# A Fourier-operator kernel on one NeuronCore: the order of the interleaved fc1 and fc2 steps, and the place of one addition, in the spectral mixing of layers 1 to 3

## The chip, the cores and the metric

The kernel runs on one core of one Trainium2 chip. The metric is the device time of one execution in microseconds (us); lower is better. The engines are TensorE (PE in the profile; PEld is its weight load), VectorE (DVE), ScalarE (ACT), GpSimd (POOL) and SyncE (SP, which here only issues DMAs). PSUM is the memory that TensorE writes and that VectorE and ScalarE empty[...].

## The reference, cut to what matters

Eight images of 8 channels, 256 x 256, in fp32. Each is normalised in 4 groups, goes through a small Fourier neural operator (4 layers, 4 groups of width 10, 12 x 12 complex modes), and then through fc1 (10 to 128 per group), a swish and fc2 (128 to 2 per group). The result is added to the image; a second normalisation and a 3 x 3 maximum follow.

```python
h = _gconv1x1(h, fc0_w, fc0_b)
for i in range(4):
    h1 = _spectral_conv(h, sp_w1[i], sp_w2[i])   # FFT, mix 12x12 modes over channels, inverse FFT
    h2 = _gconv1x1(h, w_w[i], w_b[i])
    h = h1 + h2
    if i < 3:
        h = _gswish(h, betas[i])
h = _gswish(_gconv1x1(h, fc1_w, fc1_b), betas[3])
return _gconv1x1(h, fc2_w, fc2_b)
...
x = x + _L0_conv_ref(_gn(x), ...)
x = x + _L1_conv_ref(_gn(x))                      # 3x3 maximum
```

## The kernel before, in words

**Two images at once.** The layers of image b and the head (fc1, swish, fc2, addition to x) of image b-1 run interleaved. The layers are written as generators. Each `yield` hands out a short string, and the main loop turns every letter of it into one step of the head of the image before. While image 0 is in its layers there is no such head, and the letters do nothing. A head has 128 fc1 steps and 64 fc2 steps.

**The letters** (function `step`, L839). `f` first issues all additions that are due (`sum_up`, L712) and then one fc1 step. `F` is one fc1 step without that. `C` is one fc2 step, whose addition is only put on the list `sums_due`; `c` is the same, with the additions issued directly behind it. `t` is a step of the 3 x 3 maximum of an earlier image.

**One fc1 step** (`first`, L743): 4 matmuls of 32 x 128 weights with 512 columns (8 records in the profile, since fp32 shows as two each) into a small accumulator of one PSUM bank (tag "one") and a large one of three banks (tag "tri"), L753. ScalarE empties these with two Silu activations, L754 (the small one) and L755 (the large one), into an `act` tile, of which there are 4. Every third step also issues the load of a piece of the stored state on SP's queue (L729).

**One fc2 step** (`second`, L758): 8 matmuls (16 records, L770) over the `act` tiles of two fc1 steps, into one small accumulator. **The addition** (`add`, L774) reads this accumulator on VectorE and adds it to the image's rows: L779, or L777 for every eighth. Every eighth is followed by statistics (L785) and a store on GpSimd's queue.

**The accumulators.** There are two buffers with tag "one" and two with tag "tri", shared by fc1, fc2 and the layers' own stages. Which of the two a tile gets is settled when the program is built; a matmul that gets a buffer waits for the last reader of its former content.

**The order of work.** PE, DVE, ACT and SP run in the order in which the program issues (`manual_schedule`, L860). So a step's place among the yields is its place in these queues.

**The mixing** (`mix`, L390) multiplies the 12 x 12 modes with the layer's complex weights. It is VectorE work: 6 pairs of a multiplication (L398) and a reduction (L401), then six small sums and differences (L416, L417). The counter `n` runs over these 12 operations, and for layers 1 to 3 the string handed out behind operation n is:

```python
elif n not in (0, 2, 6, 10):
    yield "CF" if n in (1, 4, 7, 9) else "f"
```

Behind the small sums stands `yield "fc"` (L418), and then TensorE's fold of the modes (L429). Ahead of the mixing stands `spectrum_h` (L353), whose strings are "fc", "f", "fc", "f", "fc", "f"; its last TensorE work, L379, lies between that last "f" and the mixing. `sum_up` runs in an `f` ahead of its fc1 step, so an addition put on the list at n = 1 is issued at n = 3.

Of the kernel before, what the change touches and what calls it, by code (L numbers as in the profile page):

```python
# [40 lines left out]
STEPS = 128  # L41
# [4 lines left out]
def fno_dilate_kernel(ctx: ExitStack, tc: tile.TileContext, a: dict, out: bass.AP):  # L46
# [17 lines left out]
    def ps_four(name):  # L64
        one, tri = ps_a(f"{name}_0"), ps_tri(f"{name}_1")
        return one, tri, [one] + [tri[:, i, :] for i in range(3)]

    def part(i):
        return slice(32 * i, 32 * i + 32)
# [5 lines left out]
    def load_x(b):  # L75
        for i in range(2):
            nc.sync.dma_start(turned[:, i], a["xw"][b, :, i])
# [89 lines left out]
    for i in range(2):  # L167
        for r in range(4):
            mm(p[part(r), 1, NO * G * i : NO * G * (i + 1)], fc0c[:, i, :], wbd[:, NO * r : NO * (r + 1), :],
               start=True, stop=True)  # L170
# [214 lines left out]
    def load_sw(l, k):  # L385
        t = sb.tile([128, G, 2 * WID, WID], F32, tag="sw", bufs=3)
        nc.sync.dma_start(t.rearrange("p g m i -> p (g m i)"), a["spw"][l, k])
        return t

    def mix(b, l, out_):  # L390

        s = [sb.tile([128, 3, 2, WID, G], F32, tag=f"S{i}", bufs=1, name=f"S{i}_{b}_{l}") for i in range(2)]
        bt, sw = out_["bt"], out_["sw"]
        for n in range(12):
            k, k2 = n // 4, n // 2 % 2
            pr = turned[:, 2, 1024 * k2 : 1024 * k2 + 800].rearrange("p (g m i) -> p g m i", g=G, i=WID)
            if n % 2 == 0:
                nc.vector.tensor_tensor(  # L398
                    pr, sw[k], bt[:, k2, k].unsqueeze(2).to_broadcast([128, G, 2 * WID, WID]), ALU.mult)
            else:  # L400
                nc.vector.tensor_reduce(  # L401
                    s[k2][:, k].rearrange("p s o g -> p (s o) g"),
                    pr.rearrange("p g m i -> p m g i"), AX.X, ALU.add,
                )
            if l == 0:
                if n % 2 or n > 7:
                    yield
            elif n not in (0, 2, 6, 10):
                yield "CF" if n in (1, 4, 7, 9) else "f"
            if n == 2 and l == 3 and b + 1 < n_img:  # L410
                load_x(b + 1)
        for i, (x, y, op) in enumerate((
                (s[0][:, :, 0], s[1][:, :, 1], ALU.subtract), (s[0][:, :, 1], s[1][:, :, 0], ALU.add),
                (s[1][:, :, 1], s[0][:, :, 0], ALU.subtract))):
            three = [t[:, :, :9].rearrange("p k (r o) g -> p k r (o g)", r=3) for t in (x, y)]
            nc.vector.tensor_tensor(fs[:, 0:3, i].rearrange("p r k o g -> p k r (o g)"), *three, op)  # L416
            nc.vector.tensor_tensor(fs[:, 3, i, :, 0], x[:, :, 9], y[:, :, 9], op)  # L417
        yield "fc"  # L418

        n_f = 6 * NO * G  # L420
        if l > 0:
            nc.vector.tensor_copy(fz[:, :, :, 24], cz[:, l])
        if l < 2:
            nc.vector.tensor_copy(fz[:, :, :, 25], cz[:, 4 if l == 0 else 3])
        one, tri, banks = ps_four(f"p_f_{b}_{l}")
        for term in range(2):
            for r in range(4):
                for q in range(4):
                    mm(banks[q][part(r), :n_f], fold[part(q), term, :],  # L429
                       fs[part(q), r, term : term + 2].rearrange("p t k o g -> p (t k o g)"),  # L430
                       start=term == 0, stop=term == 1)
        if l == 0:
            mr = out_["mr"]
            nc.vector.tensor_tensor(dc[:, 0:1], mr[:, 0:1], mr[:, 1:2], ALU.mult)
            out_["wcn"] = sb.tile([128, 32], F32, tag="wcn", bufs=1, name=f"wcn_{b}")
            nc.vector.tensor_scalar(out_["wcn"], wc, mr[:, 1:2], None, ALU.mult)
            for r in range(4):
                mm(one[part(r), n_f : n_f + NO * G], dc, wm[:, NO * r : NO * (r + 1), :], start=True, stop=True)
        cols = fz.rearrange("p o g c -> p (o g) c")
        nc.vector.tensor_copy(  # L440
            cols[:, :, 6:24].rearrange("p x (q c) -> p q c x", q=3),
            tri[:, :, :n_f].rearrange("p q (c x) -> p q c x", c=6))
        nc.vector.tensor_copy(
            cols[:, :, 0:6].rearrange("p x c -> p c x"), one[:, :n_f].rearrange("p (c x) -> p c x", c=6))
        if l == 0:
            nc.vector.tensor_tensor(
                fz[:, :, :, 24], one[:, n_f : n_f + NO * G].rearrange("p (o g) -> p o g", o=NO), cz[:, 0], ALU.add)
# [181 lines left out]
    def start(b, out_):  # L629
        if b < n_img:  # L630
            out_["sw"] = [load_sw(0, k) for k in range(3)]
            yield from spectrum_x(b, out_)
            yield from mix(b, 0, out_)

    def rest(b, then):
        c = 0 if b == 0 else NCH - 4
        for n, _ in enumerate(then):
            yield REST[b > 0][n]
            for _ in range(2 if b == 0 else 1):
                if c < NCH:  # L640
                    read_x(b + 1, c)
                    c += 1
        for i in range(c, NCH):
            read_x(b + 1, i)

    def layers(b, stored, d, then):

        for l in range(4):
            if l > 0:
                yield from spectrum_h(b, l, d)
                yield from mix(b, l, d)
            yield from rows_of(b, l, then)
            yield from layer(b, l, d, stored, then)
        yield "stored"
        yield from rest(b, then)
# [53 lines left out]
    def sum_up():  # L712

        while sums_due:
            sums_due.pop(0)()
# [123 lines left out]
    def step(kind):  # L839

        for i, (b, (done, first, second, _)) in enumerate(heads):
            if kind in "fF" and done[0] < STEPS:
                if kind == "f":
                    sum_up()
                return first()
            if kind in "cC" and 2 * done[1] < STEPS:
                second()
                if kind == "c" or 2 * done[1] == STEPS:
                    sum_up()
                if 2 * done[1] == STEPS:  # L850
                    heads.pop(i)
                    tails.append((dilate if b + 1 < n_img else dilate_last)(b, stats_of.pop(b)))
                return

    def tail():
        if tails and next(tails[0], tails) is tails:
            tails.pop(0)

    stats_of = {}
    with tc.manual_schedule(engines={PE, DVE, ACT, SP}):  # L860
        d = {}
        for _ in start(0, d):
            pass
        for b in range(n_img):
            stored = [dram.tile([128, NQ * PIX], F32, tag=f"hs{c}", name=f"stored_{b}_{c}") for c in range(NCH)]
            ahead, new, n_ready = {}, None, 0
            for n in layers(b, stored, d, start(b + 1, ahead)):
                if n == "ready":
                    if new is None:
                        if b + 1 < n_img:  # L870
                            stats_of[b] = sb.tile([128, 8, 6], F32, tag="bn_y", name=f"bn_y{b}")
                        else:
                            stats_of[b] = spare[:, 16384:16480].rearrange("p (n s) -> p n s", s=6)
                        new = head(b, stored, stats_of[b])
                    new[3](n_ready)
                    n_ready += 1
                elif n == "stored":
                    heads.append((b, new))
                    alone[0] = False
                else:  # L880
                    for kind in n or "":
                        if kind == "t":
                            tail()
                        elif heads:
                            step(kind)
            d = ahead
        while heads:
            for kind in "ffc":
                if heads:
                    step(kind)  # L890
            tail()
        for t in tails:
            for _ in t:
                pass
# [163 lines left out]
```

## Time and profile before

| what | value |
|---|---|
| median of 3 runs | 3826.1 us (3812.43 to 3826.25) |
| the profiled execution | 3819.83 us, span 3818.0 us |
| TensorE, weight load | 3567.4 us busy, 1299.9 us |
| VectorE, ScalarE | 2422.9 us, 2821.9 us |
| fc1: matmuls L753 | 1150.2 us busy, 8192 records |
| fc2: matmuls L770 | 1024.3 us busy, 8192 records |
| activations L755, L754 | 1493.3 us, 616.3 us, 1024 each |
| additions L779 | 392 with mean 683 ns (and 56 more for the last image) |
| mixing: L398, L401 | 188.7 us, 188.9 us, 192 each |

The profile is of one execution. A row of the page gives line, engine, operation, tiles and shapes, then busy time and the mean of one, then the idle time of the engine just ahead of these instructions and what ended it. Busy times of TensorE are of overlapping matmuls whose ends are modelled, so the distance between starts says more than a length. A timeline puts neighbouring instructions of one kind into one row, and shows the idle time only ahead of the first.

### The profile page before, as it was taken

To read this page: it belongs to the slowest core of one execution; us is meant where nothing else is said; L and a number is where in the kernel's file an instruction comes from. 1 tells how busy PE (TensorE), PEld (TensorE's weight loads), DVE (VectorE), ACT (ScalarE), POOL (GpSimd) and SP (SyncE) were. 2 spreads that over 40 slices of the span, in tenths; PEclk is the share of its full clock that TensorE was granted. 3 is DMA by queue.
4 is the path that set the end of the run, shared out by engine and by line. 5 is a ranking of instruction groups with operands and counts; after the bars stand their busy time and mean duration, and the time that the engine had idled before them with its cause. 6 is when DMAs were issued, how large, how long until landed. Compare 5 with 4: busy or idle time off the path is not lost.

```text
span 3818.0 us, 117724 instructions
## 1 busy us (share of the span) xinstructions
PE 3567.4 (93%) x53432; PEld 1299.9 (34%) x53432; DVE 2422.9 (63%) x3781; ACT 2821.9 (74%) x2919; POOL 117.1 (3%) x202
## 2 busy tenths in 40 slices
PE   5768999999999999999999999999999999999997
PEld 2323333333333333333333333333333333333222
DVE  6776665557775667756776577765777566772443
ACT  2435777777777777787777877777777777778986
POOL 1000000000000000000000000000000000000000
PEclk7878999999999999999999999999999999999998
DMA  3005111432225212362123512144222532225221
GB/s 87 15 31 191 49 45 47 147 113 62 73 84 174 82 57 70 99 193 61 49 67 111 185 56 66 53 150 138 59 73 66 174 91 67 67 67 178 79 86 49
DMA packets 114067, 344.91 MB, mean 90 GB/s; under 512 B 15984, under 2 KB 18480, under 8 KB 98144
## 3 DMA queue, kind: packets, MB, share of 16 engines
q1 hardware_dynamic: 95392, 276.32, 24.0%
q0 software_dynamic: 18176, 61.07, 5.0%
q8 instruction: 420, 6.88, 0.8%
q14 instruction: 79, 0.65, 0.1%
HBM read 213.33 MB, written 123.74 MB: 88 GB/s over the span
## 4 chain that ended last, share of the span: by engine, by line
PE 74%; DVE 14%; ACT 5%; issue 4%; DMA 2%; POOL 0%; ACTq 0%; DVEq 0%; POOLq 0%
PE p_fc L770 21%; PE p_fc L753 20%; PE p_z L551 9%; PE p_z L548 7%; PE p_d L516 7%; PE p_z L545 3%; DVE turned L499 3%; PE p_u L530 3%; DVE S L401 2%; ACT act L755 2%; DVE turned L398 2%; DVE y L779 2%; PE p_g L468 2%; DMA yin<-y_rows 2%; ACT act L754 1%
## 5 line engine op out<-in xcount | busy, mean ns | idle before, releaser
L755 ACT ACTIVATE act<-p_fc 128x1536 f32<-128x1536 f32 x1024 | 1493.3, 1458 | 0.0
L753 PE MATMUL p_fc<-hs,c_w 32*128 32x512 f32 x8192 | 1150.2, 626 | 50.1 <-ACT act L754 19.1
L770 PE MATMUL p_fc<-act,c_w 128*32 128x512 f32 x8192 | 1024.3, 602 | 8.2 <-DVE y L779 6.3
L754 ACT ACTIVATE act<-p_fc 128x512 f32<-128x512 f32 x1024 | 616.3, 602 | 417.7 <-PE p_fc L753 408.4
L499 DVE STREAM_TRANSPOSE turned<-h 128x1024 f32<-128x1024 f32 x528 | 632.3, 1225 | 183.0 <-ACT h L556 182.4
L556 ACT ACTIVATE h<-p_z 128x512 f32<-128x512 f32 (+1 forms) x528 | 512.0, 1021 | 226.5 <-PE p_z L551 226.5
L779 DVE TENSOR_TENSOR y<-p_fc,y 128x512 f32<-128x512 f32 x392 | 267.6, 683 | 589.1 <-PE p_fc L770 586.4
L753 PEld LDWEIGHTS p_fc<-hs,c_w 32*128 32x128 f32 x8192 | 363.3, 184 | 638.9 <-ACT act L754 269.8
L770 PEld LDWEIGHTS p_fc<-act,c_w 128*32 128x32 f32 x8192 | 226.5, 109 | 709.8 <-issue 323.1
L551 PE MATMUL p_z<-c_binv,zt 32*128 32x256 f32 x5632 | 411.7, 406 | 0.0
L548 PE MATMUL p_z<-h,c_wt 32*32 32x512 f32 x8448 | 374.3, 607 | 8.4 <-ACT act L754 4.2
L551 PEld LDWEIGHTS p_z<-c_binv,zt 32*128 32x128 f32 x5632 | 259.6, 187 | 311.6 <-issue 298.4
L516 PE MATMUL p_d<-turned,c_fw 32*32 32x480 f32 (+1 forms) x9216 | 308.3, 540 | 0.7 <-DVE turned L499 0.4
L520 ACT ACTIVATE turned<-p_d 128x1440 f32<-128x1440 f32 x144 | 183.1, 1271 | 90.2 <-PE p_d L516 87.0
L558 ACT ACTIVATE h<-p_z,c_bias 128x512 f32<-128x512 f32 (+1 forms) x176 | 186.6, 1111 | 77.9 <-PE p_z L551 77.8
L208 DVE COPY zt<-p_g 128x264 f32<-128x264 f32 x304 | 155.4, 610 | 70.3 <-PE p_g L468 52.7
L401 DVE TENSOR_REDUCE S<-turned 128x80 f32<-128x800 f32 x192 | 188.9, 984 | 5.9
L398 DVE TENSOR_TENSOR turned<-t,B 128x800 f32<-128x800 f32 x192 | 188.7, 983 | 0.9
L516 PEld LDWEIGHTS p_d<-turned,c_fw 32*32 32x32 f32 x9216 | 127.2, 103 | 165.9 <-issue 65.0
L359 DVE STREAM_TRANSPOSE turned<-zt 128x960 f32<-128x960 f32 x96 | 176.7, 1865 | 2.5
L548 PEld LDWEIGHTS p_z<-h,c_wt 32*32 32x32 f32 x8448 | 94.3, 103 | 188.8 <-DVE y L779 54.1
L530 PE MATMUL p_u<-turned,c_stack 128*32 128x480 f32 (+1 forms) x1152 | 136.7, 543 | 11.5 <-DVE turned L519 6.2
(186 smaller groups left out, 1704.2 us busy)
## 6 DMA issues: line engine op xcount, KB each, us to landing
stored<-h SPq DMA_DIRECT2D x88, 1024.0 KB
hs<-stored SPq DMA_DIRECT2D x352, 256.0 KB
t<-in_spw SPq DMA_DIRECT2D x96, 400.0 KB
yin<-y_rows POOLq DMA_DIRECT2D x56, 512.0 KB, 5.3
h<-in_xp SPq DMA_DIRECT2D x352, 48.0 KB
turned<-in_xw SPq DMA_DIRECT2D x16, 1024.0 KB
y<-in_x SPq DMA_DIRECT2D x56, 256.0 KB
y_rows<-y POOLq DMA_DIRECT2D x56, 256.0 KB, 2.5
```

Of the source, the lines that this page charges most:

```text
L398: nc.vector.tensor_tensor(pr, sw[k], bt[:, k2, k].unsqueeze(2).to_broadcast([128, G, 2 * WID, WID]), ALU.mult)
L401: nc.vector.tensor_reduce(s[k2][:, k].rearrange("p s o g -> p (s o) g"), pr.rearrange("p g m i -> p m g i"), AX.X, ALU.add,)
L499: nc.vector.transpose(dst[:, 2 * i : 2 * i + 2], h[:, c, 2 * i : 2 * i + 2].rearrange("p f (s x) -> p f s x", s=2))
L516: mm(banks[q][part(v % 4), : 240 * n], fw8[part(q), v, :], t[part(q), :, :, v, : NBLK * WID], start=v < 4, stop=v >= 4)
L548: mm(o, wt[part(q), l, g, :], h[part(q), c, f, :], start=True, stop=False)
L551: mm(banks[q][:, HW * s : HW * (s + 1)], zt[part(q), 2 * c + s].rearrange("p f o -> p (f o)"), binv[part(q), :], start=False, stop=s == 1)
L556: nc.scalar.activation(dst, src, AF.Silu)
L753: mm(banks[g], w1[part(g), blk, :], hs[k][part(g), :], start=True, stop=True)
L754: nc.scalar.activation(act[:, 0, :], one, AF.Silu)
L755: nc.scalar.activation(act[:, 1:4, :], tri, AF.Silu)
L770: mm(acc[part(g), :], w2[:, g, 15 - rb - i : 47 - rb - i], act[:, g, :], start=i == 0, stop=i == 1)
L779: nc.vector.tensor_tensor(y, sums, y, ALU.add)
```

## The change

In the mixing of layers 1 to 3 the string at n = 1 becomes "fc", and at n = 4, 7 and 9 it becomes "fC"; the others stay "f". So in each of these four places the fc1 step is issued ahead of the fc2 step, not behind it. The fc1 step now comes with `sum_up` ahead of it, where the list is empty each time. At n = 1 the small c issues the fc2's addition directly behind it: behind the first pair of mixing operations, not behind the second. The other additions keep their places: behind n = 5, 8 and 11. The letter `F` is no longer used and goes out of `step`; a dictionary of the main loop gets another name.

```diff
             elif n not in (0, 2, 6, 10):
-                yield "CF" if n in (1, 4, 7, 9) else "f"
+                yield {1: "fc", 4: "fC", 7: "fC", 9: "fC"}.get(n, "f")
...
-            if kind in "fF" and done[0] < STEPS:
-                if kind == "f":
-                    sum_up()
+            if kind == "f" and done[0] < STEPS:
+                sum_up()
                 return first()
...
-            ahead, new, n_ready = {}, None, 0
-            for n in layers(b, stored, d, start(b + 1, ahead)):
+            nxt, new, n_ready = {}, None, 0
+            for n in layers(b, stored, d, start(b + 1, nxt)):
...
-            d = ahead
+            d = nxt
```

## The prediction

> **What bounds the kernel now.** I read the page first: the engine totals, the clock row, the chain that ended last.
>
> ```profile
> PE 3567.4 (93%) x53432; PEld 1299.9 (34%) x53432; DVE 2422.9 (63%) x3781; ACT 2821.9 (74%) x2919; POOL 117.1 (3%) x202
> PEclk7878999999999999999999999999999999999998
> PE 74%; DVE 14%; ACT 5%; issue 4%; DMA 2%; POOL 0%; ACTq 0%; DVEq 0%; POOLq 0%
> ```
>
> TensorE is the bound, at full clock after the first image. But a busy average says nothing about the stage that changes, so I took the timeline of TensorE over one mixing (image 1 of 0 to 7, layer 3). Columns: start, length, engine, line; in brackets the idle time before it and who ended that.
>
> ```profile
> 679.65 1.93 PE L770 MATMUL p_fc<-act,c_w 128*32 128x512 f32 x16
> 681.50 1.14 PE L753 MATMUL p_fc<-hs,c_w 32*128 32x512 f32 x8
> 683.37 1.14 PE L753 MATMUL p_fc<-hs,c_w 32*128 32x512 f32 x8 [0.73 <-ACT act L754]
> 684.81 1.92 PE L770 MATMUL p_fc<-act,c_w 128*32 128x512 f32 x16 [0.30 <-DVE y L779]
> 686.66 2.02 PE L753 MATMUL p_fc<-hs,c_w 32*128 32x512 f32 x16
> 688.62 2.25 PE L770 MATMUL p_fc<-act,c_w 128*32 128x512 f32 x16
> 690.80 2.01 PE L753 MATMUL p_fc<-hs,c_w 32*128 32x512 f32 x16
> 692.74 2.27 PE L770 MATMUL p_fc<-act,c_w 128*32 128x512 f32 x16
> 694.94 2.93 PE L753 MATMUL p_fc<-hs,c_w 32*128 32x512 f32 x18
> 698.09 1.13 PE L753 MATMUL p_fc<-hs,c_w 32*128 32x512 f32 x6 [0.22 <-ACT act L755]
> 699.15 1.92 PE L770 MATMUL p_fc<-act,c_w 128*32 128x512 f32 x16
> 701.01 0.41 PE L429 MATMUL p_f<-fs,c_fold 32*32 32x72 f32 x31
> ```
>
> L770 is one fc2 step, eight L753 records are one fc1 step. The stage runs from 679.65 to the fold (L429) at 701.01: 21.36 us for 5 fc2 and 9 fc1. The same stretch is 21.29 to 21.30 us (from the last matmul before it) in all 21 mixings that have an image to interleave. Read starts, not lengths, for the price of a step: an unhindered fc2 holds the queue for 1.85 (684.81 to 686.66), an fc1 pair for 1.96 (686.66 to 688.62), a single fc1 for about 0.98. So the work is 5 x 1.85 + 4 x 1.96 + 0.98 = **18.07 us, and 3.29 us are stalls**: the second fc1 comes 1.87 after the first, not 0.96 (+0.91: it waits for ScalarE to empty the accumulator that the first had just filled); fc2 at 684.81 +0.45 (for an addition that stands behind two mixing pairs on VectorE); the third and fourth fc2 take 2.18 and 2.20 (+0.33, +0.35); the run of three fc1 takes 4.21, not 2.92 (+1.29: no large accumulator free). The third fc2's excess is seen in the timeline of the weight loads:
>
> ```profile
> 689.50 0.11 PEld L770 LDWEIGHTS p_fc<-act,c_w 128*32 128x32 f32 x1 [0.32 <-issue]
> 689.81 0.15 PEld L770 LDWEIGHTS p_fc<-act,c_w 128*32 128x32 f32 x6 [0.20 <-ACT act L755]
> ```
>
> The second half of that fc2 waits for the activation of the fc1 only one before the latest. The order that the change makes is already in the trace, right ahead of this mixing (TensorE's timeline, transposes of the spectrum), with its additions delayed by VectorE's transposes:
>
> ```profile
> 665.98 1.92 PE L770 MATMUL p_fc<-act,c_w 128*32 128x512 f32 x16
> 667.83 2.02 PE L753 MATMUL p_fc<-hs,c_w 32*128 32x512 f32 x16
> 669.78 1.92 PE L770 MATMUL p_fc<-act,c_w 128*32 128x512 f32 x16
> 671.64 2.42 PE L753 MATMUL p_fc<-hs,c_w 32*128 32x512 f32 x16
> 673.99 1.92 PE L770 MATMUL p_fc<-act,c_w 128*32 128x512 f32 x16
> ```
>
> One round (fc2 and two fc1) takes 3.80 where the addition is punctual, 4.21 where a transpose (1.86) stands in front of it. The fc1 behind an fc2 starts at once (1.85), so it does not use that fc2's accumulator.
>
> [...] the first fc2's addition ran at 684.07, 2.5 us after its fc2 released TensorE at 681.50, because two mixing pairs stood ahead. [...] the 0.73 us gap stands in each of the 21 mixings. [...] The clock reads 1.00 in every mixing that I asked for, so there is nothing to win or lose there.
>
> **The change, part by part.** No instruction is added or dropped. Image 0's mixings have nothing to interleave, and layer 0's are not edited, so 7 images x 3 layers = 21 places count.
>
> (a) fc1 ahead of fc2. Four pairs per mixing swap on TensorE. Before the mixing one fc1 has just been issued, so the order fc2 fc1 fc1 ... fc1 fc1 fc1 fc2 becomes fc1 fc2 fc1, fc1 fc2 fc1, ..., fc1 fc2: the run of three at the end goes, and a pair stands at its beginning, parted by small matmuls. Each fc2 has 4, not 3, activations ahead, so it needs those at least two fc1 back.
>
> (b) The first addition moves from behind the second pair of mixing operations to behind the first pair. On VectorE it now waits for its fc2, with the other ten mixing operations queued behind it; the fold waits for those.
>
> I lay (a) and (b) out on a clock that is zero at 679.65. Prices: fc2 1.85 on TensorE, and its addition may start 1.99 after it (684.81 to 686.80); fc1 0.96 before an fc1, 0.99 before an fc2; an fc1's small accumulator is free 1.87 after its start if ScalarE is idle (681.50 to 683.37); ScalarE takes 1.82 per fc1 (687.82 to 689.64); a mixing pair 1.92, an addition 0.60 of queue and 0.69 to its result. Hand-over 0.06.
> - fc1 at 0.00, fc2 at 0.99, fc1 at 2.85 (first accumulator free at 1.87: **the 0.91 goes**).
> - First addition: VectorE is there at 2.50, the data at 2.98: it waits 0.48, ends 3.67. fc1 at 3.81 needs that accumulator: free. **The 0.45 goes.**
> - fc2 at 4.80, fc1 at 6.66. The second addition could start at 6.79 but stands behind the next pair until 7.43; it ends 8.12, so the fc1 due at 7.61 starts at 8.18: **new stall 0.56**.
> - fc2 at 9.17, its addition at 11.16 to 11.85 (data, not queue, late); fc1 11.03 and 11.99; fc2 12.98; fc1 14.83. **The 0.33 and 0.35 go**: its activations are ready at 11.7, before 12.98.
> - The statistics (0.73) push the fourth addition to 15.33; it ends 16.08 and the fc1 due at 15.79 starts 16.13, when ScalarE has also just given back a large accumulator (16.07): **0.34 remains of 1.29**.
> - fc2 17.12, fold 18.98. VectorE is through at about 16.9, two us earlier, so (b)'s wait is covered; without that cover it would cost its 0.48.
>
> Per mixing 21.36 - 18.98 = **2.38 us; x 21 = 50 us**.
>
> (c) Bounds. If the second and fourth addition are punctual, all 3.29 go: 69 us. If the builder hands each second fc1 an accumulator that ScalarE frees, not the one of the addition, it waits 0.9 in each of four rounds and 0.3 us or less is gained, possibly 0.3 lost: the reason not to take this is that the fc1 at 687.54 (weight load) began 0.05 us after an addition's end, before ScalarE's pass at 687.82. I take 2.38.
>
> (d) The queues passed. fc1 issues its state load on SP every third time; the fc1 numbers keep their places among the yields, and no y load falls into these mixings, so SP's order is unchanged. The store of y on POOL stays behind its addition. `nxt` is a rename, the lost "F" branch was not otherwise used: nothing.
>
> (e) What is late next. ScalarE's backlog at the fold: 0.84 after it against 0.69 now; the fc1 behind the fold waits for the last addition in both cases (0.88 after the fold). So nothing is handed back there that I can see, at most 0.15 x 21 = 3 us, inside the range. ScalarE's 3.64 per round stays under TensorE's 3.80.
>
> **Sum.** Profiled execution 3819.8 (span 3818.0 and 1.8 around it) - 50 = 3769.8. The median of the runs, 3826.1, lies 6.3 above the profiled one; I predict midway, 3773.
>
> **Rivals.**
> - *Half of it*: additions come late in every round, as at 671.64, where the round took 4.21. Four rounds at +0.41 leave 3.29 - 1.64 = 1.65 per mixing, 35 us: about 3788. For it: VectorE is busy 15.8 of 21.3 us here. Against: its mixing pieces are half as long as those transposes.
> - *Given back*: the fold comes early, but a load or ScalarE then holds up what follows; or the builder's buffers trade stalls one for one. Within 0.9 us per mixing: about 3820. Against: the wait list has no line of fc1 waiting for its state load, and the DMA share is 0.2 to 0.4.
> - *Slower*: the fc1 behind each fc2 gets that fc2's own accumulator. Then it starts 1.99 + 0.69 + 0.06 = 2.74 after the fc2, not 1.85: 4 x 0.89 = 3.56, more than the 3.29 removed, +0.27 x 21 = 6 us, about 3829 from the midpoint; with each addition behind one more reduction (0.96) four times that again, up to +4.1 x 21 = 86 us. It decides from a mean stall of 0.82 per round. Against: 1.85 at 665.98 to 667.83.
> - *Nothing happens* cannot be: both queues' orders change.
>
> **Numbers.** Forecast (1.9 to 3.3 us per mixing) 0.67; half 0.13; given back 0.12; slower 0.08. About 0.5% (19 us, 0.9 us per mixing) can be told from no change. Faster: forecast and half, 0.80; slower's small form counts as same, so same 0.15, slower 0.05. The range goes from 3750 (all stalls gone) to 3803, past the half case; the two last cases are left out.
>
> **What would show it.** In TensorE's timeline of a mixing: fold 19.0 after its beginning; no stall at the second fc1; one of about 0.5 before the sixth fc1 put down to L779; fc2 at 1.85 each. VectorE's first addition 0.5 idle. Wrong if the fc1 behind an fc2 starts 2.7 after it, or if the fold is early and the stage behind it longer.

## The result, and the profile after

| | before | after |
|---|---|---|
| median of the runs | 3823.3 us (4 runs: the three of "Time and profile before" and one more) | 3776.4 us (4 runs) |
| profiled execution, its span | 3819.8, 3818.0 us | 3774.5, 3772.7 us |
| stretch from the last matmul ahead of a mixing to its fold, 21 mixings | 21.29 us each, 447.1 in all | 19.10 us each, 401.1 in all |
| span without these stretches | 3370.9 us | 3371.6 us |

The ratio of after to before is 0.9884, 95% interval 0.9862 to 0.9907: 1.2% faster, a small difference but clear of the noise. The last two rows are worked out from the starts and ends in the two traces: the span fell by 45.3 us, the 21 stretches by 46.0 us. So the gain lies in the stage that was edited. That the rest of the span agrees to 0.7 us is partly luck: up to the first of the 21 mixings the kernel after took 4.7 us longer (453.2 for 448.5), and behind it, outside the stretches, 4.0 us less. In the traces of experiments 1 to 5, where the same steps only change places, this rest lies between 3366.1 and 3382.3 us. Nothing larger than such differences was handed back.

The page after, the engine totals and the clock row:

```profile
PE 3539.5 (94%) x53432; PEld 1290.1 (34%) x53432; DVE 2423.5 (64%) x3781; ACT 2824.0 (75%) x2919; POOL 117.3 (3%) x202
PEclk7878999999999999999999999999999999999998
```

The instruction counts are those of before, and so is the clock row. TensorE's busy time falls by 27.9 us; VectorE's and ScalarE's change by 2.1 us at most. The change cannot be read from these sums. Over one mixing TensorE counts as busy for 20.05 of 21.30 us before and for 18.60 of 19.10 us after (windows 679.7 to 701.0 and 679.9 to 699.0): since the ends of matmuls are modelled, two thirds of the time that was saved had been counted as busy.

TensorE's timeline after, the same mixing (image 1, layer 3):

```profile
679.86 1.14 PE L753 MATMUL p_fc<-hs,c_w 32*128 32x512 f32 x8
680.93 1.92 PE L770 MATMUL p_fc<-act,c_w 128*32 128x512 f32 x16
682.79 2.02 PE L753 MATMUL p_fc<-hs,c_w 32*128 32x512 f32 x16
684.74 1.92 PE L770 MATMUL p_fc<-act,c_w 128*32 128x512 f32 x16
686.59 1.14 PE L753 MATMUL p_fc<-hs,c_w 32*128 32x512 f32 x8
688.11 1.14 PE L753 MATMUL p_fc<-hs,c_w 32*128 32x512 f32 x8 [0.37 <-DVE y L779]
689.18 1.92 PE L770 MATMUL p_fc<-act,c_w 128*32 128x512 f32 x16
691.03 2.02 PE L753 MATMUL p_fc<-hs,c_w 32*128 32x512 f32 x16
692.98 1.92 PE L770 MATMUL p_fc<-act,c_w 128*32 128x512 f32 x16
694.84 2.41 PE L753 MATMUL p_fc<-hs,c_w 32*128 32x512 f32 x16
697.18 1.92 PE L770 MATMUL p_fc<-act,c_w 128*32 128x512 f32 x16
699.03 0.88 PE L429 MATMUL p_f<-fs,c_fold 32*32 32x72 f32 x64
```

From its beginning at 679.86 to the fold it is 19.17 us, for 21.36. Every fc2 holds the queue for 1.85 to 1.86; the third and fourth were 2.18 and 2.20. The second fc1 follows the first fc2 at once (682.79 is 1.86 after 680.93). One stall is new: 686.59 to 688.11 is 1.52 where a pair that nothing hinders has 0.96, and it is put down to the addition L779. The last pair takes 2.34 up to its fc2 (694.84 to 697.18), for 1.96.

VectorE's timeline after shows the two additions that matter:

```profile
682.92 0.69 DVE L779 TENSOR_TENSOR y<-p_fc,y 128x512 f32<-128x512 f32 x1 [0.47 <-PE p_fc L770]
...
687.37 0.68 DVE L779 TENSOR_TENSOR y<-p_fc,y 128x512 f32<-128x512 f32 x1
```

The first, now directly behind its fc2, waits 0.47 for it. The second has no idle time ahead of it: VectorE reached it late, behind a reduction.

Whom TensorE waited for, in the whole execution (total us, times, longest), of before:

```profile
PE p_fc L753 <- ACT act L754: 19.1, 42, 0.7
PE p_fc L753 <- DVE y L779: 13.0, 20, 1.8
PE p_fc L770 <- DVE y L779: 6.3, 21, 0.3
```

and of after, where the line of fc2 (L770) has gone, and fc1 waits for an addition 21 times more, once per mixing:

```profile
PE p_fc L753 <- ACT act L754: 3.9, 21, 0.2
PE p_fc L753 <- DVE y L779: 20.8, 41, 1.8
```

These idle times count from the modelled end of a matmul, so they are less than the start-to-start loss (0.37 against 0.56 above).

### The profile page after: what moved, and what is told of

The parts are those of the page before. It is cut to its first block, busy times and chain, and to the rows that moved or that the text cites. A ratio compares the mean times of both kernels' runs of the same rounds, so it can differ in the third digit from the quotient of the medians.

```text
span 3772.7 us, 117724 instructions
## 1 busy us (share of the span) xinstructions
PE 3539.5 (94%) x53432; PEld 1290.1 (34%) x53432; DVE 2423.5 (64%) x3781; ACT 2824.0 (75%) x2919; POOL 117.3 (3%) x202
## 4 chain that ended last, share of the span: by engine, by line
PE 72%; DVE 16%; issue 5%; ACT 4%; DMA 2%; POOL 0%; ACTq 0%; DVEq 0%; POOLq 0%
PE p_fc L770 19%; PE p_fc L753 19%; PE p_z L551 9%; PE p_z L548 7%; PE p_d L516 7%; PE p_z L545 3%; DVE y L779 3%; PE p_u L530 3%; DVE turned L499 3%; DVE S L401 3%; DVE turned L398 2%; PE p_g L468 2%; DMA yin<-y_rows 2%; DVE turned L359 1%; PE p_b L368 1%
## 5 line engine op out<-in xcount | busy, mean ns | idle before, releaser
L753 PE MATMUL p_fc<-hs,c_w 32*128 32x512 f32 x8192 | 1136.3, 626 | 40.6 <-DVE y L779 20.8
L770 PE MATMUL p_fc<-act,c_w 128*32 128x512 f32 x8192 | 1009.3, 601 | 1.6 <-issue 1.5
L779 DVE TENSOR_TENSOR y<-p_fc,y 128x512 f32<-128x512 f32 x392 | 267.9, 683 | 537.6 <-PE p_fc L770 537.6
L770 PEld LDWEIGHTS p_fc<-act,c_w 128*32 128x32 f32 x8192 | 221.8, 109 | 701.2 <-issue 321.3
```

The lines of the kernel that those rows point to most:

```text
L753: mm(banks[g], w1[part(g), blk, :], hs[k][part(g), :], start=True, stop=True)
L770: mm(acc[part(g), :], w2[:, g, 15 - rb - i : 47 - rb - i], act[:, g, :], start=i == 0, stop=i == 1)
L779: nc.vector.tensor_tensor(y, sums, y, ALU.add)
```

## The experiments

**The theory.** In the old order, stalls came from three places: an fc1 that had to wait for the accumulator of the fc1 just ahead of it, an fc2 that needed an activation only one fc1 old, and three fc1 in a row at the end. The swap ends most of them. The early first addition keeps the new order fed with accumulators. **The rival** says that the punctual addition did it, and the order is by the way. Two more questions are whether VectorE's wait is really covered, and what a late addition costs. Per mixing, "stretch" is the one of the table above (before 21.29, after 19.10).

**1. The swap alone.**

```diff
-                yield {1: "fc", 4: "fC", 7: "fC", 9: "fC"}.get(n, "f")
+                yield {1: "fC", 4: "fC", 7: "fC", 9: "fC"}.get(n, "f")
```

> The swap alone: fc1 ahead of fc2 in all four places, the first addition left behind the second pair of mixing operations. Stretch from the last matmul ahead of the mixing to the fold; 21.29 us before, 19.10 after the whole change. Order theory (the stalls went because the fc1 behind each fc2 takes an accumulator emptied long ago, and fc2 needs older activations): about 19.4 to 19.6, since only the third fc1 waits some 0.3 to 0.9 longer for its accumulator and the second addition's stall partly absorbs it; 7 to 10 us slower than the whole change, about 38 us faster than before. Addition theory (the punctual first addition is what freed the accumulators): 20.8 or more, under 12 us of the gain.

Measured: stretch 19.83 in 20 mixings, 19.82 in one; median 3795.9 us, ratio to before 0.992 (0.9898 to 0.9941). TensorE's timeline (image 1, layer 3):

```profile
680.45 1.14 PE L753 MATMUL p_fc<-hs,c_w 32*128 32x512 f32 x8
682.68 1.14 PE L753 MATMUL p_fc<-hs,c_w 32*128 32x512 f32 x8 [1.10 <-DVE y L779]
```

One stall of 1.27 (2.23 for 0.96) is there: the third fc1 gets the accumulator of the first fc2, whose addition stands behind two mixing pairs. The swap alone brings 1.46 of the 2.19 us. I expected 19.4 to 19.6, with 0.3 to 0.9 of wait at the third fc1; the wait of 1.27 was underrated. The four swaps were not tried one by one: which stall each of them ends is read from the timelines.

**2. The first addition alone**, in the old order.

```diff
-                yield "CF" if n in (1, 4, 7, 9) else "f"
+                yield {1: "cF", 4: "CF", 7: "CF", 9: "CF"}.get(n, "f")
```

> The first addition alone: it stands directly behind its fc2, but the order stays fc2 ahead of fc1. Order theory: the first fc1 pair waits 0.45 rather than 0.91, the second fc2 no longer 0.45, the later 0.33, 0.35 and 1.29 stay: about 20.4 to 20.9 per mixing, some 8 to 18 us faster than before. Addition theory: near 19.3, some 42 us faster than before.

Measured: stretch 20.74 to 20.75; median 3810.4 us, ratio 0.9964 (0.9953 to 0.9974). It brings 0.55 of 2.19. Swap 1.46, addition 0.55, both 2.19: the sum of the parts is 2.01, and 0.18 comes only from having both. The order brings most of the gain; the addition is worth a quarter in the old order and a third (0.73) in the new.

**3. All additions direct, in the old order**, the strongest form of the rival.

```diff
-                yield "CF" if n in (1, 4, 7, 9) else "f"
+                yield "cF" if n in (1, 4, 7, 9) else "f"
```

> The old order (fc2 ahead of fc1) with all four additions directly behind their fc2. Order theory: the order's own stalls stay (an fc2 needs the activation of the fc1 one before the latest, 0.33 each; three fc1 in a row at the end, 1.3), so 20.4 to 20.8 per mixing. Addition theory (all of it is about punctual additions): 18.7 to 19.1, as in the new order with all additions direct (18.66).

Measured: stretch 20.45; one run, 3804.3 us, beside 3821.4 of before. TensorE's timeline (image 1, layer 3) keeps the order's own losses:

```profile
693.27 2.25 PE L770 MATMUL p_fc<-act,c_w 128*32 128x512 f32 x16
695.46 2.01 PE L753 MATMUL p_fc<-hs,c_w 32*128 32x512 f32 x16
...
699.60 2.93 PE L753 MATMUL p_fc<-hs,c_w 32*128 32x512 f32 x18
...
703.81 1.92 PE L770 MATMUL p_fc<-act,c_w 128*32 128x512 f32 x16
```

The fc2 at 693.27 still takes 2.19, and the run of three fc1 still 4.21 (699.60 to 703.81), as before. With all four additions direct, the old order is 1.35 us slower per mixing than the change, and 1.79 us slower than the new order with all four direct (experiment 4). The rival falls.

**4. All additions direct, in the new order.**

```diff
-                yield {1: "fc", 4: "fC", 7: "fC", 9: "fC"}.get(n, "f")
+                yield "fc" if n in (1, 4, 7, 9) else "f"
```

> The new order with all four additions directly behind their fc2, as the first one is. Order and accumulator theory: the 0.54 us stall ahead of the third pair shrinks to about 0.3 (0.28 of it waiting for ScalarE's large accumulator or the punctual addition), the last one to 0.3; but VectorE then waits for four fc2 steps with the mixing operations queued behind, so that it is through only at about 18.2, close to the fold: about 18.6 to 18.8 per mixing, 8 to 10 us faster than the change. Rival (VectorE's waits become the bound): fold later than 19.1, so slower than the change.

Measured: stretch 18.66, as expected; median 3773.4 us, ratio 0.9862 (0.9846 to 0.9879). TensorE's timeline (image 1, layer 3) shows that the sixth fc1's stall has shrunk: its pair now takes 2.23 to the next fc2 (683.06 to 685.29), not 2.59 (686.59 to 689.18 in the change).

```profile
683.06 2.31 PE L753 MATMUL p_fc<-hs,c_w 32*128 32x512 f32 x16
685.29 1.93 PE L770 MATMUL p_fc<-act,c_w 128*32 128x512 f32 x16
```

Since its interval overlaps that of the change, I ran both again side by side.

> The changed kernel once more, beside the version with all four additions direct, on the same chip. By the stage 46 us faster than before, ratio 0.988.

> All four additions direct, beside the changed kernel. By the stage 18.66 against 19.10 in 21 mixings, so 9 us faster than the changed kernel, ratio to before 0.9855 to 0.986. If it is within 3 us of the changed kernel, the gain of the stage is handed back elsewhere.

Measured: 3776.3 us, ratio 0.9887 (0.9871 to 0.9904) for the change, and 3769.8 us, 0.9865 (0.9847 to 0.9882) for all direct. In both pairs of traces the stage is 0.44 us shorter in each of the 21 mixings, 9.2 us in all; the medians say 3.0 and 6.6 us, where I had expected 9, and the intervals still overlap. In the profiled executions themselves the 9.2 us do not arrive: the span without the 21 stretches is 3379.3 and 3382.3 us with all additions direct, against 3371.6 and 3371.7 us for the change. TensorE also had a granted clock of 0.5 for longer there: 54.6 and 47.8 us from the first of these mixings until 80 us ahead of the end, against 23.9 and 30.7 (mean over the span 0.971 and 0.972, against 0.973 and 0.974). Whether the direct additions cause this is not shown. So the stage is better; that the kernel is faster is not shown.

**5. Additions late, in the new order**: each one fc1 step later than in experiment 1, behind n = 4, 7 and 9 and the small sums.

```diff
-                yield "CF" if n in (1, 4, 7, 9) else "f"
+                yield "fC" if n in (1, 4, 7, 9) else "F"
```

> The new order with every addition issued one fc1 step later than in the change (behind n = 4, 7, 9 and the small sums, no longer behind n = 1, 5, 8 and 11). It tests the price of a late addition and where the gain is used up. If an addition's lateness passes to TensorE through the accumulator that the next fc1 needs, stalls of about 0.9, 0.3 and 0.6 come back: about 20.4 to 20.6 per mixing, near 28 us slower than the change and still 17 us faster than before. If the accumulators do not bind in the new order: 19.1 as in the change. If the slower rival's mechanism sets in (each fc1 gets the accumulator of its own fc2): 22 or more.

Measured: stretch 20.75 to 20.76 in 7 mixings, 22.34 to 22.43 in 14; median 3824.7 us, ratio 1.0002 (0.9989 to 1.0015). In its timeline of TensorE, a mixing of the first kind (image 2, layer 1):

```profile
909.97 1.14 PE L753 MATMUL p_fc<-hs,c_w 32*128 32x512 f32 x8
913.12 1.14 PE L753 MATMUL p_fc<-hs,c_w 32*128 32x512 f32 x8 [2.00 <-DVE y L779]
```

and one of the second kind (image 1, layer 1):

```profile
457.25 1.83 PE L753 MATMUL p_fc<-hs,c_w 32*128 32x512 f32 x8 [2.00 <-DVE y L779]
459.02 2.88 PE L770 MATMUL p_fc<-act,c_w 128*32 128x512 f32 x16
```

The first kind confirms the price of a late addition: it comes back as a stall of the next fc1 (2.19 start to start beyond the 0.96), and the stretch is near the 20.4 to 20.6 that I expected. The second kind has the same 2.00 of idle time, but the matmuls behind it take 1.83 and 2.88, not 1.14 and 1.92. The reason stands in the table of stretches, in the column ahead of the last two (after start, length, and busy time with count for PE, PEld, DVE, ACT, POOL):

```profile
457.20:460.60 3.40, 3.35 (x16) 0.71 (x20) 2.78 (x3) 1.47 (x3) 0.00 (x0) 0.56 0.10 23
...
913.10:916.50 3.40, 3.38 (x28) 1.04 (x32) 3.06 (x4) 1.94 (x2) 0.00 (x0) 1.00 0.25 56
```

TensorE's granted clock is 0.56 behind the stall in one mixing (457.20 to 460.60) and 1.00 in the other (913.10 to 916.50); over the stretches it is 0.92 (451.3 to 473.6) and 1.00 (907.1 to 927.8). In this profiled execution 14 of 21 mixings thus pay another 1.6 to 1.7 us, 23 us in all. At 20.75 each the 21 stretches would be 11 us shorter than before (I expected 17); with the slow clock they are 11.7 us longer, 458.8 for 447.1.

What sets these 14 apart from the other seven, which have the same 2.00 of idle time, is not shown.

**6. More work on VectorE**, between the last reduction and the small sums of the changed kernel. It multiplies the last weights again and writes the same values.

```diff
+        for _ in range(2 if l > 0 else 0):
+            nc.vector.tensor_tensor(
+                pr, sw[k], bt[:, k2, k].unsqueeze(2).to_broadcast([128, G, 2 * WID, WID]), ALU.mult)
```

> The changed kernel with two redundant multiplications (the last one again, 0.98 us each) on VectorE between the last reduction and the small sums of each mixing of layers 1 to 3. In the changed kernel VectorE is through 2.2 us ahead of the fold. Cover theory (VectorE is off the path there, so the first addition's wait of 0.47 costs nothing): fold at 19.10 as before, the 3 mixings of image 0, where VectorE is the bound, 1.96 longer each (14.8 for 12.83), in all some 6 us. Rival (VectorE's queue is the path): 21.1 per mixing, 41 us more.

> The same with four. Cover theory: the cover of 2.2 us is used up, so 3.92 - 2.2 = 1.7 to 1.8 us come through: fold at 20.8 to 20.9; image 0's mixings 3.92 longer. [...]

Measured, one run each, beside 3821.4 of before. With two: stretch 19.10 in all 21 mixings, image 0's three at 14.76 to 14.77 for 12.83; 3780.2 us. With four: 20.69 on average of the 21, a little under what was expected, image 0's at 16.82; 3813.1 us. Whom TensorE waited for at the fold (total us, times, longest), with two:

```profile
PE p_f L432 <- DVE fs L420: 44.3, 3, 14.8
```

and with four:

```profile
PE p_f L432 <- DVE fs L420: 82.3, 24, 16.8
```

With 1.96 us more of VectorE per mixing the fold waits for it only in image 0's 3 mixings. With 3.92 it waits in all 24. So the cover is real, and the 0.47 that the first addition waits is free here. It is 2.33 us, a little more than the 2.2 expected: of 3.92 only 1.59 came through. The idle time ahead of the late fold is 1.52 us. The stretch ends at the fold and cannot show what the clock does behind it. In the timeline of one mixing (image 1, layer 3) that goes on behind it, the fold holds the queue for 0.85 (714.00 to 714.85), against 0.88 in the change (699.03 to 699.91).

## Why the prediction was right

It said 3773 (3750 to 3803); the median is 3776.4. By its own steps:

- **The 3.29 us of stalls per mixing.** Right, and so is where they lay: the four that the prediction said would go have gone, in each of the 21 mixings. (Its five parts add up to 3.33, since the prices are rounded.)
- **The starting point.** It lay midway between one profiled time and a median of three, at 3823. The median of four runs is 3823.3: that was luck, since the three runs alone spread over 14 us.
- **(a) The swap.** Right. fc1 at 2.85 after the beginning: measured 2.93. fc2 at 4.80: 4.88. fc1 at 6.66: 6.73. The new stall of 0.56 at the sixth fc1: measured 0.56 (1.52 - 0.96). The rest at the ninth of 0.34: measured 0.30 (its weight load starts at 696.10, due at 695.80, and is put down to the addition L777).
- **(b) The addition's wait.** Right: 0.47 measured for 0.48, and the cover held (experiment 6). The first addition of before ran 2.57 us after its fc2 had released TensorE, not 2.5. What the prediction left open is what the early addition is worth: without it, 0.73 of the 2.19 goes (experiment 1).
- **The sum.** 2.38 per mixing was forecast, 2.19 is measured; 50 against 46 us. The term that was too small is an fc1 that stands between a stall or other work and an fc2: I took 0.99, and it is 1.07 (679.86 to 680.93, 688.11 to 689.18) and 1.08 at the third such place. Three times 0.08 to 0.09 is 0.25, of which 0.04 came back at the ninth fc1. The lines of the prediction had it: the last fc1 of before, 698.09 to 699.15, takes 1.06, though this row has only six of its eight records.
- **(c) Who gets which accumulator.** The choice taken held: the fc1 behind an fc2 never waited for that fc2's addition. The next one did, and in experiment 5 it did so although the other small accumulator was free sooner: ScalarE had emptied that of the fc1 at 909.97 by 911.73, and the next fc1 still waited for the addition, which ended at 913.06, until 913.12. So the accumulator is fixed by the program, not by who is ready.
- **(e) Nothing is handed back.** Right just behind the stage: from the fold to the next stage's first matmul (L468) it is 4.70 us in both kernels.
- **The clock.** "At full clock after the first image" was read from a page whose slices are 95 us long. The clock records of before have a granted clock of 0.5 six times between 798 and 2310 us, for 30.7 us in all. None of it lies in the 21 mixings, so the forecast did not suffer.
- **The rivals.** *Half of it* and *given back* did not come. *Slower* named the fc2's own accumulator; that did not happen in any run. But experiment 5 shows another road there, which I had ruled out by saying that the clock can neither win nor lose: behind a stall of 2.0 us another 1.6 to 1.7 us were lost in 14 of 21 mixings, at a granted clock of 0.56 in the one whose window is shown.

## What to carry to other kernels

When a bound engine is fed by two others, read the distance between starts in the one stage that changes, and price each step by its unhindered distance. What is left are stalls, each with a buffer or a result behind it. An order in which a consumer needs results two steps old, not one, and in which no three producers of the same buffer follow each other, ended most of them here without any added instruction. Where an engine has a measured reserve (here 2.33 us of VectorE), let it wait early and give buffers back at once.

## What the runs showed of the hardware

At one place of this program, behind a stall of 2.00 us on TensorE, the stretch was 1.6 to 1.7 us longer in 14 mixings than in the other seven (experiment 5). In the two whose windows are shown the granted clock behind the stall was 0.56 in the longer one and 1.00 in the shorter. Behind stalls of 1.10 us (experiment 1) the stretch was the same to 0.01 us in all 21 mixings, and behind 1.52 us (experiment 6) the fold of the one mixing read took 0.85 us, against 0.88 in the change, where no stall stands ahead of it. The idle time was 2.00 us in the 14 and in the seven alike; why only the 14 were longer is not shown.
